# Four chained cross-attention layers: sums by products with ones in odd grouped steps alone, and ScalarE's copy of a grouped half ahead of the last masked exponentials

## The chip, the core and the metric

The kernel runs on one core of a Trainium2 chip. The core has a matrix engine (TensorE, PE in the profile, with its weight loads shown as PEld), a vector engine (VectorE, DVE), an activation engine (ScalarE, ACT), a general engine (GpSimd, POOL) and a queue that issues transfers (SyncE, SP). Each engine works through its own instructions in the order in which they stand, and waits for others by semaphores. Matrix products land in PSUM, eight banks of 128 x 512 fp32, from where ScalarE or VectorE takes them to SBUF. The metric is the device time of one launch in microseconds, the median of the timed runs.

## The reference

A state x (4 batches of 512 positions, 256 channels) goes through four cross-attention layers over one context per batch (1024 positions, 512 channels). Layers 0, 2 and 3 are alike: 16 heads of 64, a bias on the columns of a few tokens that comes from two masks over the 512 positions, softmax, product with the values, output projection, bias and residual.

```python
q = hidden_states @ Wq; k = encoder_hidden_states @ Wk; v = encoder_hidden_states @ Wv
logits = einsum('bhqd,bhkd->bhqk', q, k) * scale + col_bias
probs = softmax(logits, axis=-1)
out = einsum('bhqk,bhkd->bhqd', probs, v) @ Wo + bo + residual
```

Layer 1 normalises x by its root mean square and has 16 heads of 16 with 4 shared key and value heads, without masks. All is computed in fp32.

## The kernel before

**Units and steps.** The work is cut into units: the units of layers 0, 2 and 3 ("masked" units), eight to a layer and batch, two heads each; and the units of layer 1 ("grouped" units), also eight to a batch. The main loop (L1227) runs over steps. A step takes one masked unit `g`, and in four stretches of eight steps, one for each batch, a grouped unit `lam` beside it. In the step in which `lam` is attended, the logits of the next grouped unit, `coming`, are made. A grouped unit has a half `h`: units 0, 2, 4, 6 (`h == 0`) stand in what are called even steps here, units 1, 3, 5, 7 in odd steps. `tabled[0]` is true in a step that has both `lam` and `coming`, so for units 0 to 6 of each batch: 28 steps of the 32.

**Tiles.** The logits of a unit are eight blocks of 128 x 1024 (context positions by two heads of 512 queries). All the rest goes over these: copy to SBUF, maximum, subtraction, exponential in place, products with the values.

**A step in the order of the code.**
- POOL subtracts the maximum from the blocks of `lam` (L952).
- TensorE makes the scores of `g` (`scores`, L849), ScalarE copies each block to SBUF (L859), VectorE takes maxima (L906 and the small operations to L946).
- TensorE attends the masked unit of the step before, `g1` (`attend`, L882).
- Then a list `fill` of matrix work is run: output projections (L1086), queries (L746), keys of the next masked units (L540) in odd steps or values (L588) in even steps. Beside it, ScalarE and VectorE get their work from a list `events`: each entry has a time in microseconds of estimated matrix work, and `pass_events(us)` issues what lies before it. For `g` these are eight subtractions (L954) at 0.7 + 1.2 t and eight exponentials (L960) at 3.3 + 1.22 t, with a running sum on POOL behind each exponential (L999). After each piece of matrix work that leaves a result to be copied, the loop calls `pass_events(now)` and then issues the copy (L1443 to L1447).
- Where the estimates in `fill` pass 9.5, `attend_grouped` (L1392) is put in: the attention of `lam` (L882, tiles of 32 columns). It returns `keep_even` (L887), so the loop first issues the exponentials that are due and then ScalarE's copy of one half of the result into `o` (L892). VectorE's addition of the other half, `keep_odd` (L896), is put on the list `late`; in odd steps `turn_grouped` (L1001 to L1015) too.
- The logits of `coming` follow in four pairs of blocks (`logits_pair`, L822), with a piece of `fill` between two pairs. Each pair takes two places of two banks; `Place` (L109) picks among banks 0 to 3 in these steps, so a pair uses the banks of the pair before. ScalarE copies both blocks (L828), VectorE takes their maxima (L906). Before the first pair, `behind_exponentials` (L1299) issues all remaining events and then what is on `late`.

**The sums of the softmax.** For `g1` the running sum of its exponentials is added over 128 partitions. There are two ways. `sums_beside` (L1050) does it with two matrix products with ones (L1054), put in `fill` in front of `attend_grouped`; VectorE then turns one row over, takes the reciprocal and turns it back (L785 to L787). `reciprocal_sums` (L1024) does it on VectorE alone: a reduction over the running sum (L906, on the tile `st`), seven small operations (L1031 to L1036), the reciprocal (L1040) and one turn (L1042). Both end in `scale_out` (L1068), and both are on `late`. `by_ones` (L1320) picks the first way; before the change it holds in all 28 steps.

## Time and profile before

| | us |
|---|---|
| timed runs | 3494.37, 3494.56, 3499.84; median 3494.56 |
| profiled execution | 3500.28 |
| its span, first to last instruction | 3498.5 |
| TensorE busy | 3447.4 |
| VectorE busy | 2964.0 |
| POOL busy | 2491.6 |
| ScalarE busy | 2336.4 |
| granted TensorE clock, mean | 0.996 |

A row of the costliest groups or of a timeline gives line, engine, operation, tiles, shapes and count. In the timelines here the columns are: start in us from the span's start, length in us, engine, line, operation, result and source, count of instructions merged into the row, and in brackets the idle time before it and what ended it. A list of waits has: who waited, for whom, the total in us, how often, and the longest. An fp32 matrix product shows as two instructions. Matrix products are pipelined, so the length of a row of them reaches a little into the next one; differences of starts are what the engine needed.

### The profile page before, as it was taken

Reading aid. Unit: us, or ns where it says so; the run is one execution under the profiler, and the core shown is the slowest. Engines: PE = TensorE matmul, PEld = TensorE weight load, DVE = VectorE, ACT = ScalarE, POOL = GpSimd, SP = SyncE. Lnnn points to the kernel's source line nnn. Section 1 sums busy time; section 2 is a strip of 40 time slices with the busy share of each in tenths; the row PEclk is TensorE's granted clock in tenths of the full one; section 3 lists DMA queues with packets and bytes.
Section 4 is the critical chain, followed back from the end, with each engine's and each line's share of the span. In section 5 each row is a group of like instructions: output and inputs, shape, how many; then the busy total and the mean of one; then the engine's idle time right before and its main releaser. Section 6 shows DMA issues by size and latency. Waiting matters only on the chain.

```text
span 3498.5 us, 42340 instructions
## 1 busy us (share of the span) xinstructions
PE 3447.4 (99%) x15374; PEld 1673.5 (48%) x15374; DVE 2964.0 (85%) x3898; ACT 2336.4 (67%) x2701; POOL 2491.6 (71%) x1241
## 2 busy tenths in 40 slices
PE   8999999999999999999999999999999999999998
PEld 4454444444444454444545455454544445454553
DVE  7778788887888878898888888888788888889887
ACT  4565577775777757776666666666577766666664
POOL 3665577884888848887777768777488877769774
PEclk9999999999999999999999999999999999999999
DMA  3223211002100120001001011011101101011010
GB/s 104 64 73 107 63 32 50 26 23 74 43 28 28 37 82 29 26 29 44 28 28 52 25 34 52 28 52 43 48 29 50 35 20 52 28 39 59 31 32 7
DMA packets 146198, 151.69 MB, mean 43 GB/s; under 512 B 23608, under 2 KB 123448, under 8 KB 145476
## 3 DMA queue, kind: packets, MB, share of 16 engines
q1 hardware_dynamic: 142894, 140.05, 12.7%
q0 software_dynamic: 2560, 8.39, 0.8%
q8 instruction: 122, 2.00, 0.2%
q14 instruction: 88, 0.72, 0.1%
q10 hardware_dynamic: 534, 0.52, 0.0%
HBM read 132.15 MB, written 15.73 MB: 42 GB/s over the span
## 4 chain that ended last, share of the span: by engine, by line
PE 88%; DVE 8%; ACT 2%; POOL 1%; issue 1%; DMA 0%; DVEq 0%; ACTq 0%; POOLq 0%
PE ps L882 19%; PE ps L849 17%; PE ps L643 13%; PE ps L588 11%; PE ps L540 10%; PE ps L746 5%; PE ps L822 4%; PE ps L1086 4%; DVE tops L906 2%; DVE st L954 2%; DVE ps L866 1%; POOL st L952 1%; ACT st L828 1%; PE ps L723 1%; PE ps L1054 1%
## 5 line engine op out<-in xcount | busy, mean ns | idle before, releaser
L999 POOL TENSOR_TENSOR st<-st 128x1024 f32<-128x1024 f32 x668 | 1581.7, 2368 | 682.3 <-ACT st L960 637.4
L960 ACT ACTIVATE st<-st 128x1024 f32<-128x1024 f32 x1024 | 1040.1, 1057 | 330.7 <-DVE st L954 188.4
L954 DVE TENSOR_TENSOR st<-st,ps 128x1024 f32<-128x1024 f32 x768 | 883.2, 1214 | 3.3
L952 POOL TENSOR_TENSOR st<-st 128x1024 f32<-128x1024 f32 x256 | 598.1, 2381 | 281.9 <-DVE st L946 281.9
L882 PE MATMUL ps<-st,v 128*64 128x512 f32 (+1 forms) x4064 | 791.3, 597 | 4.7 <-ACT kt L545 4.7
L866 DVE TENSOR_TENSOR ps<-ps,st 128x1024 f32<-128x1024 f32 x476 | 586.7, 1233 | 246.3 <-ACT st L859 202.9
L859 ACT COPY st<-ps 128x1024 f32<-128x1024 f32 x768 | 714.6, 1050 | 67.4 <-PE ps L855 51.3
L849 PE MATMUL ps<-qt,kt 64*128 64x512 f32 x3072 | 710.6, 600 | 10.5 <-DVE every L933 8.3
L906 DVE TRANSPOSE_TENSOR_REDUCE tops<-st 128x32 f32<-128x1024 f32 x448 | 517.7, 1211 | 55.8 <-ACT st L828 55.3
L882 PEld LDWEIGHTS ps<-st,v 128*64 128x64 f32 (+1 forms) x4064 | 240.1, 130 | 541.1 <-issue 456.1
L849 PEld LDWEIGHTS ps<-qt,kt 64*128 64x128 f32 x3072 | 285.0, 186 | 377.0 <-ACT st L859 153.9
L540 PE MATMUL ps<-ctx,wk 128*128 128x512 f32 x896 | 414.4, 610 | 2.2 <-ACT ctx L420 2.2
L588 PE MATMUL ps<-wv,ctx 128*128 128x256 f32 x1792 | 405.9, 382 | 0.0
L588 PEld LDWEIGHTS ps<-wv,ctx 128*128 128x128 f32 x1792 | 336.2, 190 | 96.7 <-issue 48.0
L828 ACT COPY st<-ps 128x1024 f32<-128x1024 f32 x256 | 247.2, 1017 | 108.0 <-PE ps L822 107.7
L540 PEld LDWEIGHTS ps<-ctx,wk 128*128 128x128 f32 x896 | 168.4, 193 | 236.8 <-issue 220.3
L643 PE MATMUL ps<-st 128*128 128x128 f32 (+1 forms) x1200 | 228.9, 339 | 5.2 <-ACT ps L666 5.2
L658 ACT COPY st<-ps 128x512 f32<-128x512 f32 x40 | 23.4, 586 | 301.6 <-PE ps L643 301.6
L643 PEld LDWEIGHTS ps<-st 128*128 128x128 f32 x1200 | 158.8, 192 | 73.4 <-issue 66.2
L746 PE MATMUL ps<-x,wq 128*128 128x512 f32 x384 | 186.6, 609 | 1.1 <-ACT x L383 1.1
L822 PE MATMUL ps<-qt,kt 32*128 32x512 f32 x1024 | 170.1, 640 | 8.7 <-ACT st L828 8.3
L1086 PE MATMUL ps<-ot,wo 128*128 128x512 f32 x384 | 175.8, 600 | 0.7 <-DVE ot L1068 0.7
(184 smaller groups left out, 2694.8 us busy)
## 6 DMA issues: line engine op xcount, KB each, us to landing
ctx<-kept SPq DMA_DIRECT2D x24, 1024.0 KB, 8.1
wk<-in_L_xattn_Wk_dram SPq DMA_DIRECT2D x47, 512.0 KB, 3.5
wv<-in_L_xattn_Wv_dram SPq DMA_DIRECT2D x47, 512.0 KB, 3.4
wq<-in_L_xattn_Wq_dram SPq DMA_DIRECT2D x96, 128.0 KB, 3.5
wo<-in_L_xattn_Wo_dram SPq DMA_DIRECT2D x96, 128.0 KB, 3.5
st<-kept SPq DMA_DIRECT2D x4, 2048.0 KB
qt<-q SPq DMA_DIRECT2D x64, 128.0 KB, 3.5
kept<-st SPq DMA_DIRECT2D x12, 512.0 KB, 3.2
```

The lines of the kernel that those rows point to most:

```text
L540: nc.tensor.matmul(m, lhsT=g.w["k"][:, k, :], rhs=ctx_half[g.b, n][:, k, :], start=(k == 0), stop=(k == KT - 1),)
L588: nc.tensor.matmul(m[:, half * 2 * P : (half + 1) * 2 * P], lhsT=ctx_half[g.b, t // 4][:, k, t % 4 * P : (t % 4 + 1) * P], rhs=g.w["v2"][: ...
L643: nc.tensor.matmul(m if is_keys else m[:, q], lhsT=right[:, k, :] if is_keys else left_[:, k, q], rhs=left_[:, k, :] if is_keys else right ...
L849: nc.tensor.matmul(m[:, j * S : (j + 1) * S], lhsT=g.kt[g.rows[j], keys], rhs=g.qt[g.rows[j], :], start=True, stop=t > 0,)
L859: nc.scalar.copy(g.st[t], m)
L866: nc.vector.tensor_tensor(top, top, g.st[t], ALU.max)
L882: nc.tensor.matmul(g.po[at, :], lhsT=g.v[:, t, rows], rhs=g.st[t][:, j * S : (j + 1) * S], start=(t == first), stop=(t == last),)
L906: nc.vector.tensor_reduce(out_, of.rearrange("p (b x) -> p b x", x=32), AX.X, op, apply_transpose=True)
L952: nc.gpsimd.tensor_tensor(g.st[t], g.st[t], g.mb, ALU.subtract)
L954: nc.vector.tensor_tensor(g.st[t], g.st[t], g.mb, ALU.subtract)
L960: nc.scalar.activation(st, st, AF.Exp)
L999: nc.gpsimd.tensor_tensor(g.acc, g.st[0] if t == 1 else g.acc, g.st[t], ALU.add)
```

## The change

Two edits in the main loop. The products with ones are used only where the grouped unit that is attended has `h == 1`; in the even steps of the 28 the sums of `g1` go by `normalise` (`reciprocal_sums` and `scale_out`). And `attend_grouped` no longer returns `keep_even` for the loop to issue behind the events that are due; it issues events up to 8.6 itself (subtractions to block 6, exponentials to block 4) and then the copy at once. The exponentials of blocks 5 to 7 that have not been issued by then follow the copy.

```diff
-        by_ones = tabled[0]
+        by_ones = tabled[0] and lam.h == 1
...
                 late.append(lambda: keep_odd(lam))
                 if lam.h == 1:
                     late.append(lambda: turn_grouped(lam))
-                return lambda: keep_even(lam)
+                pass_events(8.6)
+                keep_even(lam)
```

In the instruction order of the two programs this is: TensorE has 16 pairs of products with ones less and is otherwise unchanged; VectorE has ten instructions in place of three at 16 places; ScalarE's copy L892 stands in front of three exponentials (L960) that it followed before, in all 32 steps but seven, where it is one (unit 4 of each batch) or two; POOL's and SP's order is the same.

## The prediction

> **What bounds the kernel now.** I read the page first: busy shares, then the chain that ended last.

> ```profile
> PE 3447.4 (99%) x15374; PEld 1673.5 (48%) x15374; DVE 2964.0 (85%) x3898; ACT 2336.4 (67%) x2701; POOL 2491.6 (71%) x1241
> ...
> PE 88%; DVE 8%; ACT 2%; POOL 1%; issue 1%; DMA 0%; DVEq 0%; ACTq 0%; POOLq 0%
> ```

> TensorE idles 51 of 3498.5 us and carries 88% of the chain, so work taken from it should count, unless something makes it wait. Next, the waits, for who stands between the engines around the grouped unit:

> ```profile
> DVE o L896 <- ACT o L892: 48.5, 28, 2.7
> ...
> PEld ps L822 <- ACT st L828: 47.6, 62, 2.3
> ```

> VectorE waits 48.5 us for the half copy (L892) that the change moves forward. TensorE in its turn waits for the pair copies (L828), which stand behind L892 on ScalarE. So the timelines of an even step (unit 2 of batch 0), TensorE then ScalarE then VectorE:

> ```profile
> 559.65 1.08 PE L1054 MATMUL ps<-st,ones 128*64 128x512 f32 x4
> 560.66 3.64 PE L882 MATMUL ps<-st,v 128*32 128x512 f32 x32
> 564.23 1.14 PE L822 MATMUL ps<-qt,kt 32*128 32x512 f32 x8
> 565.30 1.99 PE L588 MATMUL ps<-wv,ctx 128*128 128x256 f32 x8
> 567.23 1.34 PE L822 MATMUL ps<-qt,kt 32*128 32x512 f32 x8
> 568.50 1.99 PE L588 MATMUL ps<-wv,ctx 128*128 128x256 f32 x8
> ```
> ```profile
> 560.14 2.96 ACT L960 ACTIVATE st<-st 128x1024 f32<-128x1024 f32 x3
> 564.37 0.58 ACT L892 COPY o<-ps 64x512 f32<-64x512 f32 x1 [1.27 <-PE ps L882]
> 565.46 1.93 ACT L828 COPY st<-ps 128x1024 f32<-128x1024 f32 x2 [0.51 <-PE ps L822]
> ```
> ```profile
> 560.78 0.72 DVE L785 STREAM_TRANSPOSE ot<-ps 128x512 f32<-128x512 f32 x1 [1.88 <-PE ps L1054]
> ...
> 564.98 0.69 DVE L896 TENSOR_TENSOR o<-o,ps 64x512 f32<-64x512 f32 x1 [1.72 <-ACT o L892]
> ```

> See three things. ScalarE does its three exponentials while TensorE still runs the grouped attention, and only then waits for it. VectorE is idle 1.88 + 1.72 us. And the second pair (567.23) has to wait for the first pair's copies, since both use banks 0 to 3: TensorE goes on at 568.50, which is 3.04 us after the first copy's start. The odd step (unit 3) has the same constant, with an open wait:

> ```profile
> 604.36 1.46 PE L822 MATMUL ps<-qt,kt 32*128 32x512 f32 x8
> ...
> 609.17 2.04 PE L822 MATMUL ps<-qt,kt 32*128 32x512 f32 x8 [1.43 <-ACT st L828]
> 611.14 3.64 PE L540 MATMUL ps<-ctx,wk 128*128 128x512 f32 x4
> ```
> ```profile
> 604.52 2.95 ACT L960 ACTIVATE st<-st 128x1024 f32<-128x1024 f32 x3
> 607.50 0.58 ACT L892 COPY o<-ps 64x512 f32<-64x512 f32 x1
> 608.10 1.93 ACT L828 COPY st<-ps 128x1024 f32<-128x1024 f32 x2
> ```

> Here 611.14 - 608.10 = 3.04 again. So the moment the first pair copy starts sets TensorE.

> **The change part by part.**

> *Sums in the 16 even steps, TensorE.* One pair of products with ones goes: 560.66 - 559.65 = 1.01 us, and TensorE runs without a gap from there to 607. By itself: 16 x 1.01 = 16.2 us less.

> [...] I go by the gapless rows.

> *Sums, VectorE.* Three instructions (0.72 + 0.25 + 0.71, with gaps 1.79) become ten, ahead of the same L1068. The row of unit 7, which has them already, runs from 778.83 (L906) to 782.56 (L1068): 3.73. Extra 1.94 us, 31.0 in all. In the even step it no longer waits for the products: its last subtraction ends at 558.9, so sums, scaling and all end near 563.4 to 564.7 (the bank for the reduction is the one ScalarE empties until 560.24). Then it needs the half copy, then the pair copies; both come later, so the cover is the 3.6 us of idle above. If that cover were gone, 1.94 a step. I take 0. It can't go below nothing either: what ends earlier on VectorE here only waits longer for the half copy at L896.

> *Half copy ahead of the exponentials.* The copy needs the end of the grouped attention; what is now queued behind that wait is three exponentials (one in the four units 4, two in two odd steps and one unit 7, by the instruction order of the two programs), and behind them the pair copies that TensorE needs. Even step, unit 2: TensorE ends the attention at 564.23 - 1.01 = 563.22; the copy starts 0.14 later (564.37 - 564.23); 0.60 to the next instruction (607.50 to 608.10); three exponentials 2.98 (604.52 to 607.50); the first pair copy starts at 566.94, not 565.46. Plus 3.04: TensorE goes on at 569.98, not 568.50, so it is **1.48 us later**, though 1.01 of work has gone. Nothing gives that back: the later pairs follow at the same distance, and the next step's VectorE and POOL work starts from the last pair. Worth it per kind:
> - units 0, 2, 6, twelve steps: eleven x 1.48 = 16.3; unit 0 of batch 1, where the first copy was at 908.06 and the attention's end at 906.56, comes to 909.27: 1.2.
> - unit 4, four steps: two of the exponentials already stand ahead, one (1.04) comes behind: attention's end 652.03 - 1.01 + 0.14 + 0.60 + 1.04 = 652.80 against 653.26: -0.46, -1.8 in all.
> - unit 5, four steps: nothing was taken from TensorE; attention's end 693.79 + 0.14 + 0.60 + 2.98 = 697.51 against 695.89: 1.62 each, 6.5.
> - units 1 and 3, eight steps: in six the attention ends when ScalarE arrives (604.36 + 0.14 = 604.50 against 604.52), so copy and exponentials only trade places: 0. In unit 1 of batch 1 and unit 3 of batch 3 TensorE came late to the attention, waiting for a key copy (L545): 950.96 + 0.14 + 0.60 + 2.0 = 953.70 against 952.19, 1.5; 2688.16 + 2.74 = 2690.90 against 2689.44, 1.5.
> - unit 7, four steps: no pair follows; the key copies come up to 1.7 later (784.97 for 783.27), but TensorE's next product rows stand unbroken from 781.25 with other banks free: 0, at most 1.7.

> What VectorE wins: its add (L896) and in odd steps the four grouped operations run up to 1.7 us sooner. That is worth nothing if it next waits for a pair copy, and it does (idle before L906 in all: 55.3 us, for L828). POOL's running sums come to the late exponentials 0.5 us after they are ready (three of 2.43 us from 558.19 put block 5's add at 565.5, its exponential ends at 565.0); were they late, nobody reads them before the next step. DMA: no issue moves or is added; SP's and POOL's queues keep their order.

> *Sum.* 16.3 + 1.2 - 1.8 + 6.5 + 1.5 + 1.5 = +25.2 us, the 16.2 already inside (the forward copy alone would be 41.4). The profiled execution took 3500.28 us, so its like would take 3525.5; it stands 5.7 above the median of the timed runs, 3494.56, and I add the difference to the median: **3519.8 us**.

> Unknown, with both ends: how long after TensorE's end the copy starts when ScalarE is already waiting, 0.14 in the row that waited 1.27; a floor is the block that the copy reads last, one of eight earlier (3.57 / 8 = 0.45): 22 steps x 0.45 = 10 less. I take 0.14, the same wait. And the six ties: from 0 to 0.6 each if TensorE slips by a copy's length, 3.6 more. I take 0, as both sides of the tie start from the same pair.

> **The rivals.**
> *Faster, the wait is hidden.* Place: the second pair. If TensorE could issue it before the copies, the 16.2 would stay whole: 3478.4. The point that decides: the first copy must start by 565.46 to break even, which leaves 565.46 - 563.96 = 1.50 for exponentials behind the half copy: one gains, two lose. For it: TensorE idles for L828 seldom today. Against: 3.04 in both steps shown, with and without an idle gap.
> *Faster, VectorE sets the odd steps.* The chain runs on VectorE from 575.7 to 606.4. If it did so after, too, twelve odd steps x 1.71 and 16.2 make 36.7: 3457.8. Against: the chain goes on over ScalarE's exponential, L892 and L828, whose sum in front of 608.10 stays the same.
> *About the same.* The late pair is made up in ScalarE's pauses (1.27 and 0.54 us between the later pairs) before the next step. Then the even steps cost nothing and save nothing, unit 5 likewise: within 7 us of 3494.6. Against: TensorE, not ScalarE, would have to catch up, and it has no pause.
> *Slower still.* VectorE's cover fails in the twelve steps, 23.3 more: 3543.

> **How the numbers follow.** My sum 0.77; slower still 0.09; about the same 0.06; hidden 0.05; VectorE 0.03. The sum's own range is 3510 (0.45 earlier) to 3530 (ties 3.6, units 7 up to 6.8). Wider by 5 for the spread of the runs (3494.37 to 3499.84), which also reaches a little into the slower case, it holds 8 in 10: 3504 to 3535. A measurement of this kernel tells about 0.2%, 7 us. Slower 0.86, same 0.06, faster 0.08.

> **What will show it.** L1054 x48 instead of x112; L785 gone from the even steps, L1031 to L1042 there. ScalarE's wait at L892 for L882, 8.6 us in all today, grows to some 45 us: 2.4 in twelve even steps, 1.6 in the units 5, the rest in the units 7 and the two late odd steps. TensorE is idle about 1.8 us before the second pair in twelve even steps (arrival 566.22, start some 1.07 after the first copy). VectorE's wait at L896 gone from most steps, and moved to L906. I am wrong if in unit 2 the first pair copy starts before the last exponential, or TensorE goes on less than 6 us after the attention's end.

## The result and the profile after

The changed kernel takes 3534.41 us (median of 4 runs, 3530.31 to 3537.66), the kernel before 3497.2 beside it: a ratio of 1.0105, 95% interval 1.0093 to 1.0117. The profiled execution takes 3535.15 us, its span is 3533.4, against 3500.28 and 3498.5 before: +34.9, where the sum of the prediction was +25.2. The mean granted clock (the share of full speed that the profile shows as granted to TensorE) fell from 0.996 to 0.990. The kernel is slower by about 1%, clear of the noise.

The page of the changed kernel, busy shares and the chain that ended last:

```profile
PE 3458.9 (98%) x15310; PEld 1678.5 (48%) x15310; DVE 2992.8 (85%) x4010; ACT 2332.4 (66%) x2701; POOL 2490.0 (70%) x1241
...
PE 89%; DVE 4%; ACT 4%; POOL 1%; issue 1%; DMA 0%; DVEq 0%; ACTq 0%; POOLq 0%
```

TensorE has 64 instructions less and is busy 11.5 us longer. That is the first thing to explain: waits lengthen its idle time (74.5 us now, 51.1 before), but less work should not lengthen its busy time.

The waits of the kernel before, then of the changed kernel (who, for whom, total us, times, longest):

```profile
ACT o L892 <- PE ps L882: 8.6, 16, 1.3
...
PE ps L822 <- ACT st L828: 8.3, 6, 1.4
```
```profile
DVE tops L906 <- ACT st L828: 96.6, 77, 4.4
...
PEld ps L822 <- ACT st L828: 80.8, 77, 2.4
...
ACT o L892 <- PE ps L882: 46.7, 26, 3.1
...
PE ps L822 <- ACT st L828: 33.2, 24, 1.6
```

ScalarE now waits 46.7 us at the half copy, 8.6 before. TensorE waits 33.2 for pair copies, 8.3 before, and 24 times, six before. Its weight loads wait for them 80.8, 47.6 before; that wait lies inside the second pair, between its two blocks, and counts as busy in a merged row (2.04 for 1.34 us), which is part of the longer busy time.

The step that the prediction worked through, unit 2 of batch 0, TensorE, then ScalarE, then VectorE:

```profile
565.72 1.14 PE L822 MATMUL ps<-qt,kt 32*128 32x512 f32 x8
566.79 1.99 PE L588 MATMUL ps<-wv,ctx 128*128 128x256 f32 x8
570.24 2.04 PE L822 MATMUL ps<-qt,kt 32*128 32x512 f32 x8 [1.45 <-ACT st L828]
572.20 1.99 PE L588 MATMUL ps<-wv,ctx 128*128 128x256 f32 x8
```
```profile
565.86 0.58 ACT L892 COPY o<-ps 64x512 f32<-64x512 f32 x1 [3.11 <-PE ps L882]
566.34 2.95 ACT L960 ACTIVATE st<-st 128x1024 f32<-128x1024 f32 x3
569.19 1.90 ACT L828 COPY st<-ps 128x1024 f32<-128x1024 f32 x2
```
```profile
562.85 1.26 DVE L906 TRANSPOSE_TENSOR_REDUCE ps<-st 128x32 f32<-128x1024 f32 x1 [1.45 <-ACT v L595]
...
566.58 0.69 DVE L1068 TENSOR_TENSOR ot<-ps,ot 128x512 f32<-128x512 f32 x1
567.30 0.69 DVE L896 TENSOR_TENSOR o<-o,ps 64x512 f32<-64x512 f32 x1
570.22 4.67 DVE L906 TRANSPOSE_TENSOR_REDUCE tops<-st 128x32 f32<-128x1024 f32 x4 [2.23 <-ACT st L828]
```

ScalarE stands 3.11 us at L892 until the attention ends (565.72), copies, does the three exponentials, and only then takes the first pair. TensorE goes on at 572.20, 6.48 us after the attention's end; before it was 4.27. The sums on VectorE wait 1.45 us at their own start, are done before the pair copy comes, and VectorE waits 2.23 us more for that copy.

**Step by step.** For each of the 32 grouped steps I took how much later the next step's scores (L849) start than in the kernel before, less the same for the step before it. Some single steps are off by about 1.70 us or twice that, either way; apart from that, each kind of step gives one number to 0.1 us: units 0, 2 and 6 +1.1 to +1.21 (unit 0 of batch 1 +0.93), unit 4 -0.69, unit 5 +1.42 to +1.49, units 1, 3 and 7 nothing within 0.1, but +1.5 and +1.3 in the two late odd ones. Together +19.8. The steps of 1.70 add up to the rest, some 15.

**Where the 1.70 comes from.** A gap is a stretch in which TensorE runs nothing. The windows of the changed kernel around two of them (stretch, length, busy time and instructions of PE, PEld, DVE, ACT, POOL, then granted clock, DMA share, GB/s), and TensorE's rows in the second:

```profile
478.00:486.00 8.00, 7.32 (x27) 4.05 (x28) 4.67 (x4) 4.35 (x6) 6.57 (x3) 0.79 0.00 0
522.00:530.00 8.00, 7.05 (x21) 2.27 (x22) 5.95 (x6) 4.37 (x7) 7.76 (x4) 0.79 0.09 33
```
```profile
519.58 1.98 PE L540 MATMUL ps<-ctx,wk 128*128 128x512 f32 x4
522.95 2.04 PE L822 MATMUL ps<-qt,kt 32*128 32x512 f32 x8 [1.39 <-ACT st L828]
524.92 3.68 PE L540 MATMUL ps<-ctx,wk 128*128 128x512 f32 x4
```

The kernel before has the same pattern at the same place:

```profile
520.50 2.10 PE L822 MATMUL ps<-qt,kt 32*128 32x512 f32 x8 [1.41 <-ACT st L828]
522.53 3.58 PE L540 MATMUL ps<-ctx,wk 128*128 128x512 f32 x4
```

In the changed kernel the same four instructions of L540 take 1.98 us ahead of the gap and 3.68 behind it. The clock is at one half for 3.41 us (0.79 over 8 us is 1 - 0.5 x 3.41 / 8; the window 525.06:528.47 shows 0.50), which costs 1.70 us of TensorE's work. In the record of the granted clock between 400 and 2950 us, where the grouped steps lie, the kernel before has 7 such stretches (23.9 us), the changed one 14 (54.6 us, two of them doubled). Half of the difference, (54.6 - 23.9) / 2 = 15.3 us, is lost. So the steps and the clock make 19.8 + 15.3 = 35.1 us, against 34.9 measured.

### The profile page after: what moved, and what is told of

It is laid out like the page before. It is cut to its first block, busy times and chain, and to the rows that moved or that the text cites. A ratio compares the mean times of both kernels' runs of the same rounds, so it can differ in the third digit from the quotient of the medians.

```text
span 3533.4 us, 42334 instructions
## 1 busy us (share of the span) xinstructions
PE 3458.9 (98%) x15310; PEld 1678.5 (48%) x15310; DVE 2992.8 (85%) x4010; ACT 2332.4 (66%) x2701; POOL 2490.0 (70%) x1241
## 3 DMA queue, kind: packets, MB, share of 16 engines
q8 instruction: 121, 1.98, 0.2%
## 4 chain that ended last, share of the span: by engine, by line
PE 89%; DVE 4%; ACT 4%; POOL 1%; issue 1%; DMA 0%; DVEq 0%; ACTq 0%; POOLq 0%
PE ps L882 20%; PE ps L849 18%; PE ps L643 13%; PE ps L540 11%; PE ps L588 10%; PE ps L822 5%; PE ps L746 5%; PE ps L1086 4%; ACT st L960 2%; POOL st L952 1%; DVE ps L866 1%; ACT st L828 1%; DVE st L954 1%; PE ps L855 1%; PE ps L723 1%
## 5 line engine op out<-in xcount | busy, mean ns | idle before, releaser
L960 ACT ACTIVATE st<-st 128x1024 f32<-128x1024 f32 x1024 | 1040.7, 1057 | 332.0 <-DVE st L954 187.9
L882 PE MATMUL ps<-st,v 128*64 128x512 f32 (+1 forms) x4064 | 793.2, 599 | 4.7 <-ACT kt L545 4.7
L849 PE MATMUL ps<-qt,kt 64*128 64x512 f32 x3072 | 710.6, 599 | 8.8 <-DVE every L933 6.5
L906 DVE TRANSPOSE_TENSOR_REDUCE tops<-st 128x32 f32<-128x1024 f32 x448 | 518.1, 1212 | 97.3 <-ACT st L828 96.6
L882 PEld LDWEIGHTS ps<-st,v 128*64 128x64 f32 (+1 forms) x4064 | 240.6, 130 | 536.4 <-issue 464.5
L849 PEld LDWEIGHTS ps<-qt,kt 64*128 64x128 f32 x3072 | 285.5, 186 | 374.8 <-ACT st L859 153.1
L540 PE MATMUL ps<-ctx,wk 128*128 128x512 f32 x896 | 417.2, 613 | 2.2 <-ACT ctx L420 1.1
L588 PE MATMUL ps<-wv,ctx 128*128 128x256 f32 x1792 | 413.7, 387 | 0.0
L588 PEld LDWEIGHTS ps<-wv,ctx 128*128 128x128 f32 x1792 | 340.9, 193 | 99.8 <-issue 43.1
L828 ACT COPY st<-ps 128x1024 f32<-128x1024 f32 x256 | 246.5, 1013 | 113.3 <-PE ps L822 113.2
L540 PEld LDWEIGHTS ps<-ctx,wk 128*128 128x128 f32 x896 | 168.9, 194 | 239.3 <-issue 223.4
L643 PE MATMUL ps<-st 128*128 128x128 f32 (+1 forms) x1200 | 228.9, 339 | 5.1 <-ACT ps L666 5.1
L822 PE MATMUL ps<-qt,kt 32*128 32x512 f32 x1024 | 184.8, 653 | 33.2 <-ACT st L828 33.2
L643 PEld LDWEIGHTS ps<-st 128*128 128x128 f32 x1200 | 158.8, 192 | 73.4 <-issue 64.0
```

The source lines that it names most:

```text
L540: nc.tensor.matmul(m, lhsT=g.w["k"][:, k, :], rhs=ctx_half[g.b, n][:, k, :], start=(k == 0), stop=(k == KT - 1),)
L588: nc.tensor.matmul(m[:, half * 2 * P : (half + 1) * 2 * P], lhsT=ctx_half[g.b, t // 4][:, k, t % 4 * P : (t % 4 + 1) * P], rhs=g.w["v2"][: ...
L643: nc.tensor.matmul(m if is_keys else m[:, q], lhsT=right[:, k, :] if is_keys else left_[:, k, q], rhs=left_[:, k, :] if is_keys else right ...
L849: nc.tensor.matmul(m[:, j * S : (j + 1) * S], lhsT=g.kt[g.rows[j], keys], rhs=g.qt[g.rows[j], :], start=True, stop=t > 0,)
L882: nc.tensor.matmul(g.po[at, :], lhsT=g.v[:, t, rows], rhs=g.st[t][:, j * S : (j + 1) * S], start=(t == first), stop=(t == last),)
L906: nc.vector.tensor_reduce(out_, of.rearrange("p (b x) -> p b x", x=32), AX.X, op, apply_transpose=True)
```

## Experiments

The medians of the kernel before lay between 3497.1 and 3498.4 us beside the experiments. "Half clock" is the time at half clock between 400 and 2950 us in the profiled execution.

| run | median us | ratio to before, 95% | half clock, us |
|---|---|---|---|
| sums alone | 3476.45 | 0.9932, 0.9916 to 0.9949 | 10.2 |
| copy alone | 3557.76 | 1.0155, 1.0133 to 1.0177 | 68.3 |
| one exponential behind | 3483.87 | 0.9957, 0.994 to 0.9973 | 6.8 |
| two behind | 3500.82 | 1.0013, 1.0003 to 1.0022 | 13.7 |
| no products at all | 3489.34 | 0.9977, 0.9967 to 0.9987 | 44.4 |
| gap filled, first try | 3556.06 | 1.017, 1.0151 to 1.0188 | 51.2 |
| gap filled, second try | 3562.97 | 1.0197, 1.0181 to 1.0212 | 47.8 |
| longer piece in the gap | 3513.22 | 1.0043, 1.0029 to 1.0057 | 6.8 |
| longer piece elsewhere | 3571.18 | 1.021, 1.0192 to 1.0228 | 54.6 |
| copy behind the pair | 3478.48 | 0.9945, 0.9927 to 0.9963 | 6.8 |
| the same, odd steps alone | 3473.34 | 0.9938, 0.9925 to 0.9952 | 0 |
| and one exponential later | 3468.49 | 0.9919, 0.9906 to 0.9933 | 6.8 |

### The two edits apart

The sums alone (against the kernel before):

```diff
-        by_ones = tabled[0]
+        by_ones = tabled[0] and lam.h == 1
```

> Only the first edit: in even steps the sums go by VectorE, the half copy stands where it stood. Theory (TensorE is bound by when the first pair copy starts; the forward copy alone made the loss): the attention of the grouped unit ends 1.01 us sooner in 16 even steps, and the pair copies follow, except where ScalarE's exponentials then end later than the attention (idle before the half copy was 0.43 or 0.25 us, so 0.8 to 0.93 is left): about 14 us less, 3483 of a median of 3497. Rival (VectorE's extra 1.94 us a step is on the path): 0 to 31 us more, 3497 to 3528.

The copy alone (against the changed kernel):

```diff
-        by_ones = tabled[0] and lam.h == 1
+        by_ones = tabled[0]
```

> Only the second edit: products with ones in all 28 steps, the half copy ahead of the exponentials. Theory: even steps of units 0, 2 and 6 lose 0.14 + 0.48 + 2.85 + 3.01 - 4.27 = 2.2 us each (26 us), units 4 lose 0.3, units 5 1.5, two late odd steps 1.4 each: 36 us. Theory of the clock: every idle of TensorE of over 1.2 us can be followed by 3.4 us at half clock, 1.7 us lost; as many as in the changed kernel (15 against 7 in the stretch) add 14 us: 3547 in all. Rival (the two edits are bad only together): near 3497.

Sums alone: apart from the clock's 1.70, the even steps are 1.00 to 1.04 us shorter, but for unit 0 of batch 1 (0.54) and the first, which holds all that differs ahead of it (1.57); the expectation had 0.8 to 0.93 for some of them. The odd ones stay. TensorE in unit 2, with no gap between the first and the second pair:

```profile
559.98 1.14 PE L822 MATMUL ps<-qt,kt 32*128 32x512 f32 x8
561.05 1.99 PE L588 MATMUL ps<-wv,ctx 128*128 128x256 f32 x8
562.97 1.34 PE L822 MATMUL ps<-qt,kt 32*128 32x512 f32 x8
```

Copy alone: units 0, 2 and 6 come 2.21 later, unit 4 0.32, unit 5 1.47: the changed kernel's 1.21 and -0.69 with the 1.01 put back, and unit 5 as it was. ScalarE stands 4.12 us at the copy:

```profile
567.93 0.58 ACT L892 COPY o<-ps 64x512 f32<-64x512 f32 x1 [4.12 <-PE ps L882]
```

So the first edit gains and the second loses more. Both runs go further than the waits: half clock falls to 10.2 us in the one and rises to 68.3 in the other.

### How many exponentials may stand behind the copy

Against the changed kernel, one and two in place of three:

```diff
-                pass_events(8.6)
+                pass_events(10.7)      # one behind;  9.5 for two
```

> Both edits, but only the exponential of block 7 stands behind the half copy. Theory: in all 16 even steps the first pair copy starts at 0.14 + 0.48 + 0.95 = 1.57 us after the attention's end, which came 1.01 sooner: 0.7 us less a step, 11 us less; odd steps unchanged: 3486. Rival (any copy ahead of exponentials makes ScalarE lose its wait of 2 to 3 us): slower than 3497.

> Both edits, with the exponentials of blocks 6 and 7 behind the half copy. Theory: 0.14 + 0.48 + 1.9 + 3.01 - 1.01 = 4.52 against 4.27: 0.25 us more in twelve even steps, 0.7 less in the four units 4 (one behind there), 0.4 more in units 5, 1.4 in two late odd steps: 5 us more, 3502, and up to 7 us from half clocks. So the sign turns between one and two exponentials. Rival (the loss is the same wherever the copy stands ahead): near 3534.

ScalarE in unit 2 with one behind, then with two:

```profile
562.22 0.58 ACT L892 COPY o<-ps 64x512 f32<-64x512 f32 x1 [1.20 <-PE ps L882]
562.70 1.05 ACT L960 ACTIVATE st<-st 128x1024 f32<-128x1024 f32 x1
563.66 1.90 ACT L828 COPY st<-ps 128x1024 f32<-128x1024 f32 x2
```
```profile
560.73 0.58 ACT L892 COPY o<-ps 64x512 f32<-64x512 f32 x1 [2.15 <-PE ps L882]
561.21 2.00 ACT L960 ACTIVATE st<-st 128x1024 f32<-128x1024 f32 x2
563.12 1.90 ACT L828 COPY st<-ps 128x1024 f32<-128x1024 f32 x2
```

From copy to pair copy it is 1.44 and 2.39 us, and 3.33 in the changed kernel (565.86 to 569.19): 0.95 for each exponential. The steps of units 0, 2 and 6 follow: -0.69, +0.26, +1.21 against the kernel before; with none behind, the run above, -1.01. The sign turns between one and two.

### Is it the gap that halves the clock?

Two tries put 1.01 us of unused products into the gap before the second pair in the even steps of the changed kernel (this adds work that the result does not use), the first in a bank that `Place` gave, the second in one picked by hand:

```diff
+            if i == 1 and lam and lam.h == 0:
+                w = Place(1)          # second try: a bank above 3, taken past Place
+                for j in range(2):
+                    nc.tensor.matmul(w.ap[coming.rows[j], :], lhsT=ones[:, 0:64], rhs=coming.qt, start=True, stop=True)
+                w.back()
```

> The changed kernel with an unused pair of products with ones (1.01 us, nothing reads them) in each even step in the idle time ahead of the second pair of logits, so that TensorE idles 0.44 instead of 1.45 us there. Theory of the clock (idle of over 1.2 us brings half clocks): the waits stay as they are, since the second pair waits for the copies anyway, but the half clocks that come in even steps go, some 5 to 8 of 1.7 us: 8 to 13 us less than the changed kernel, 3521 to 3526, though it does more work. Rival (the half clocks have nothing to do with the idle time): 3534 again.

> The changed kernel, with a pair of products of ones and queries (1.01 us, read by nobody) ahead of the second pair of logits in the even steps, written to a bank above 3 that was given back last; the choice of banks for all other work is untouched. It adds work that the result does not use. Theory (the idle gap before the second pair brings the stretches at half clock): the second pair starts when it did, the gap falls from about 1.45 to 0.45 us, no new wait appears in the steps, and the half clock stretches that begin in even steps go; 5 to 8 of them at 1.7 us each, so 3520 to 3526. Rival (the clock falls for another reason, for instance by time or by load): gap smaller, as many half clock stretches as in the changed kernel (14, of which two double), about 3534.

Both missed. TensorE of the first try, then of the second, around unit 2:

```profile
573.50 2.03 PE L822 MATMUL ps<-qt,kt 32*128 32x512 f32 x8 [0.44 <-ACT st L828]
...
587.00 5.40 PE L849 MATMUL ps<-qt,kt 64*128 64x512 f32 x16 [2.11 <-DVE every L933]
```
```profile
573.18 1.31 PE L1311 MATMUL ps<-qt,ones 128*64 128x512 f32 x4 [2.84 <-ACT v L595]
```

In the first the gap did fall to 0.44, but `Place` gives the bank that came back longest ago, so the extra request changed the banks of all that followed, and a wait of 2.11 us arose in the next scores. In the second the bank was still being copied by ScalarE (L595), so the gap grew to 2.84. Neither tests the gap.

What does: the piece of values or keys between the first and the second pair gets two of its products twice, in its own bank and ahead of the right ones (work that the result does not use; no other instruction is added and no bank changes). A control does the same with the piece between the third and the fourth pair, where TensorE has no gap.

```diff
+        for k in range(2 if twice[0] else 0):       # v_pair; likewise in k_part
+            nc.tensor.matmul(..., start=True, stop=True)
...
             logits_pair(coming, i)
+            twice[0] = bool(lam and i == 0)          # i == 2 in the control
```

> The changed kernel, with two of the products of the piece of keys or values between the first and the second pair of logits done twice (1.0 us, in the bank that the piece owns, the first result overwritten) in all 28 steps that have pairs. It adds work and changes no other instruction. Theory (the idle gaps before the second pair bring the half clock): the second pair starts when it did, the gaps of 1.4 to 1.6 us become 0.4 to 0.6, and the 11 half clock stretches that begin behind such gaps go, three behind other waits stay: 54.6 us at half clock become some 10 to 17, so 19 to 22 us less; against it 3 us where the gap was smaller (unit 4, and two units 2 and 4): 3515 to 3519 in spite of 56 products more. Rival (the clock falls by itself, or by the load): half clock stretches as before, 3534 to 3540.

> The same 56 products, in the piece between the third and the fourth pair, where TensorE has no gap. Theory: each costs what it takes, 28 x 0.8 to 1.0 us on top of the changed kernel, with its gaps and its half clock stretches (12 to 16) kept: 3555 to 3563. If it came out near the run before it, the place of the products, and so the gap, would not be what matters.

With 56 products more, the first takes 3513.22 us, 21.2 less than the changed kernel; the second, with the same 56, takes 3571.18. The first, TensorE in unit 2 and the window over the step where the changed kernel stood at 0.79 (its lines from 588 on are numbered up to 16 higher: L604 is L588, L838 is L822, L844 is L828, L598 the products done twice):

```profile
563.12 1.13 PE L598 MATMUL ps<-wv,ctx 128*128 128x256 f32 x4
564.09 1.89 PE L604 MATMUL ps<-wv,ctx 128*128 128x256 f32 x8
566.56 2.03 PE L838 MATMUL ps<-qt,kt 32*128 32x512 f32 x8 [0.59 <-ACT st L844]
568.53 1.99 PE L604 MATMUL ps<-wv,ctx 128*128 128x256 f32 x8
```
```profile
475.00:483.00 8.00, 7.41 (x39) 4.49 (x36) 6.70 (x7) 6.55 (x8) 7.77 (x4) 1.00 0.00 1
```

TensorE goes on 6.48 us after the attention's end (568.53 - 562.05), just as in the changed kernel, so the wait is the same; the gap is 0.59 for 1.45, and the clock stays at 1.00. Half clock falls from 54.6 us to 6.8; the two stretches left stand behind other waits, in a unit 7 and a late odd step. (54.6 - 6.8) / 2 = 23.9 us, less 0.34 in each unit 4, is the 21.9 by which the profiled spans differ, but for 0.6. The control keeps the gap of 1.45 us and the half clock (3.78 us for the 1.99 of the same piece):

```profile
477.93 2.63 PE L838 MATMUL ps<-qt,kt 32*128 32x512 f32 x8 [1.45 <-ACT st L844]
480.49 3.78 PE L604 MATMUL ps<-wv,ctx 128*128 128x256 f32 x8
```

It came out above its expectation. Apart from the clock's 1.70, its steps are about 0.66 us longer than in the changed kernel where the piece is one of values (16 steps), and, where it is one of keys, 1.7 in units 1 and 3 and 1.5 in unit 5, not 0.8 to 1.0. That makes 30 us, as in the profiled spans (30.1; both have 54.6 us at half clock), and its median lies 6 above its profiled execution. That short gaps bring the half clock, and that this cost the change some 15 us, is shown by this pair of runs.

### Should the odd steps lose their products too?

```diff
-        by_ones = tabled[0]
+        by_ones = False
```

> Sums by VectorE in all 28 steps, the half copy as before the change. Theory (in odd steps ScalarE's exponentials set the first pair copy, so that TensorE's 1.01 us less only turns into idle time): the same as sums in the even steps alone, 3476, plus up to 10 us for half clocks, as the idle time ahead of the second pair in odd steps grows from 1.4 to 2.4 us. Rival (TensorE's work counts in all steps): 12 us less, 3464. Rival (VectorE is what ends the odd steps): 1.94 x 12 = 23 us more, 3499.

It is 13 us slower than the sums alone (3489.34 for 3476.45; its profiled execution, at 3494.56, is among the slowest of its ten), although TensorE has twelve pairs of products less. TensorE in unit 3 and the window over unit 1:

```profile
602.28 1.98 PE L540 MATMUL ps<-ctx,wk 128*128 128x512 f32 x4
606.29 2.04 PE L822 MATMUL ps<-qt,kt 32*128 32x512 f32 x8 [2.03 <-ACT st L828]
```
```profile
520.00:530.00 10.00, 10.00 (x30) 3.56 (x29) 9.25 (x10) 5.86 (x7) 6.22 (x3) 0.83 0.07 26
```

In the odd steps the pair copy is set by ScalarE, as the prediction read it, so the work taken from TensorE only became gap (2.03 for 1.39), and the half clock rose from 10.2 to 44.4 us, which is 17 of the difference in the profiled spans (17.1).

### The half copy the other way, behind the pair copies

If ScalarE's queue ahead of L828 sets the step, the half copy itself can leave it. First in all steps, on top of the sums alone (in unit 7, which has no pair, behind all remaining events); then in units 1, 3 and 5 only; then there with the last block's exponential behind the second pair's copies as well. The edit of the second and third run:

```diff
-        by_ones = tabled[0]
+        by_ones = tabled[0] and lam.h == 1
...
             logits_pair(coming, i)
+            for each in behind.pop(i, ()):
+                each()
...
+                if lam.h == 1 and coming:
+                    behind[0] += [lambda: keep_even(lam), lambda: keep_odd(lam), lambda: turn_grouped(lam)]
+                    pass_events(10.7)                          # third run only
+                    behind[1] += [each[2] for each in events]  # third run only
+                    events.clear()                             # third run only
+                    return
```

> Sums by VectorE in even steps, and the half copy moved the other way: behind the first pair's two copies, VectorE's additions of the grouped unit behind the pair's maxima. Theory (the start of the first pair copy sets TensorE): in odd steps it comes 0.6 us sooner, 12 x 0.6 = 7 us less than with the sums alone, 3469, and some half clocks less; in even steps nothing more than 0.2 each. Rival (the half copy holds up something else, VectorE's grouped maxima in their turn): no better than 3476, or worse.

> The kernel before with the sums by ones in odd steps alone, and in units 1, 3 and 5 the half copy, VectorE's addition and the four grouped operations behind the first pair's copies; even steps and units 7 as in the kernel before but for the sums. Theory (in odd steps ScalarE alone sets the first pair's copy, and the half copy is 0.74 us of it, as the run with the copy behind the pair showed): 12 odd steps 0.74 earlier, even steps as with the sums alone: 3476.5 - 8.9 = about 3468. Rival (the moved addition delays VectorE's maxima and gives it back in the next step): 3474 to 3478.

> As the run before it, and in the same units the exponential of the last block (1.0 us) behind the second pair's copies. Theory (ScalarE's queue ahead of the first pair's copy sets the odd steps, until the end of the grouped attention does): another 0.9 to 1.0 us in units 1 and 3 and little in unit 5, where the attention ends later: some 8 us, about 3460, and fewer gaps before the second pair, so fewer half clock stretches. Rival (the exponential delays the later copies, or the running sum of the masked unit comes late for the attention in the next step): no better than the run before it.

In all steps it gains nothing (3478.48): the odd steps are 0.74 shorter (0.6 was expected), but most even ones 0.23 longer, and in unit 7, where the copy went behind the key copies, VectorE waits for it:

```profile
DVE o L896 <- ACT o L892: 26.8, 4, 8.3
```

In odd steps alone (0.9938) it can't be told from the sums alone (0.9932). The odd steps win 0.71 to 0.76 each and most units 2, 4 and 6 behind them give 0.70 back: VectorE now has the addition and the four grouped operations between the pair's maxima and is the late one.

```profile
690.02 0.69 DVE L896 TENSOR_TENSOR o<-o,ps 64x512 f32<-64x512 f32 x1
...
693.17 6.87 DVE L906 TRANSPOSE_TENSOR_REDUCE tops<-st 128x32 f32<-128x1024 f32 x6
```

These six maxima run without a pause, so the next step's first maximum comes 3.10 us earlier than with the sums alone (703.23 for 706.33), where TensorE's scores come 3.99 earlier (699.42 for 703.41). The third run is the fastest of all, 3468.49, 0.9919 of the kernel before. Units 1 and 3 are mostly 1.65 to 1.70 shorter than with the sums alone; TensorE and ScalarE in unit 3:

```profile
597.55 1.75 PE L822 MATMUL ps<-qt,kt 32*128 32x512 f32 x8
599.23 1.98 PE L540 MATMUL ps<-ctx,wk 128*128 128x512 f32 x4
601.15 1.46 PE L822 MATMUL ps<-qt,kt 32*128 32x512 f32 x8
```
```profile
597.61 2.01 ACT L960 ACTIVATE st<-st 128x1024 f32<-128x1024 f32 x2
599.52 1.91 ACT L828 COPY st<-ps 128x1024 f32<-128x1024 f32 x2
...
604.35 1.08 ACT L960 ACTIVATE st<-st 128x1024 f32<-128x1024 f32 x1
```

The pair copy comes while TensorE still works at L540, and there is no gap. About half of what the odd steps win is still returned in units 2, 4 and 6, 0.7 each, as in the run before it.

## Why the prediction was right, and where it was not

- **What sets the step** (the first pair copy's start, TensorE going on 3.04 us behind it): right. It is 3.01 in the changed kernel with a gap in front, and the order L892, three exponentials, L828 came as written.
- **Sums, 16 x 1.01 on TensorE**: right, to 0.03 in 14 of the 16 steps of the run with the sums alone. That run is 22.8 us shorter in its profiled span, 16 of it from the steps and 6.8 from less half clock, so the gapless rows that the prediction went by held in this kernel.
- **Sums on VectorE at nothing**: right. With the sums alone the even steps lose none of their 1.01, and in the changed kernel VectorE still waits 2.23 us for the pair copy behind them.
- **Half copy, units 0, 2, 6: 1.48 each**: right in mechanism, too large by 0.27. The hand-over from the copy to an exponential took 0.48 for the 0.60 read from copy to copy, three exponentials to the pair copy 2.85 for 2.98, and the rest 3.01 for 3.04. A duration read ahead of one kind of successor was used for another. The same shows, with 0.15 to 0.23, in unit 4 (-0.69 for -0.46) and unit 5 (1.47 for 1.62). All twelve, four and four steps and the two late odd ones: 19.8 us for 25.2.
- **Ties in units 1 and 3, unit 7 at nothing**: right, within 0.1 but for the clock's steps.
- **The unknown start of the copy** (0.14, or up to 0.45 earlier): 0.14 it was, 565.86 against 565.72.
- **The missing term**: the prediction listed the idle gap before the second pair (about 1.8 us; 1.45 it became) as a sign, and priced it at its own length alone. "Nothing gives that back" was true, but a gap of this length was also followed by half clock in a good third of the cases (53 of 148 gaps of 1.3 to 1.8 us, the table at the end). The trace of before had it in full view: the 3.58 us of L540 at 522.53 behind the gap of 1.41, and the rows that the prediction itself quotes, 609.17 with 1.43 idle and 611.14 with 3.64 us for four instructions that take 1.98 elsewhere. That row was used for its start and not read for its length. Worth 15.3 us.
- **Luck in the number**: the time, 3534.41, lay 0.6 below the upper end of the range, 3535. The upper part of the range had been meant for ties, for unit 7 and for the spread of the runs; ties and unit 7 came to nothing. The forecast of 3519.8 was 14.6 short: 15.3 from the half clock, less 5.4 from the hand-overs, and the other 5 because the profiled execution of before stood 5.7 above its median and that of the changed kernel only 0.7. Had the hand-overs been sized right, forecast and range would have stood 5.4 lower and ended near 3529.6, and the time would have lain outside. The waits were understood; that the number held was luck.
- **Rivals**: "Hidden" needs the exponentials behind the half copy to take no more than 1.50 us; one takes 0.95 and gains, two take 1.9 and lose, as the prediction said. "VectorE sets the odd steps" (3457.8) is out, since odd steps with a tie did not move, and "about the same" is out, since units 0, 2 and 6 lost 1.1 to 1.21 each and made none of it up. "Slower still" had a time near the measured one for a wrong reason: the cover did not fail.

## What to carry to other kernels

Moving a short copy forward on an in-order queue moves its wait in front of all that stands behind it (ScalarE's 3.11 us at L892 in unit 2 here); count what may stand between the wait's end and the next thing the bounding engine needs (here one exponential, not two). Work taken from an engine only counts where no other queue sets its next start (1.00 to 1.04 us a step in most even steps here); where one does, the work was filling a gap (2.03 for 1.39 us in unit 3 without any products with ones), and a gap on TensorE may cost more than itself (1.70 us of clock behind one of 1.39 in the changed kernel). In the trace of before, look for the same merged row with two lengths. The longer one held either a wait (2.04 for 1.34 us at L822) or a lowered clock (3.68 for 1.98 at L540) here; the granted clock of a short window tells which (0.50 in 525.06:528.47), and what stands ahead of the second kind shows what brings it on.

## What the hardware showed that was not expected

| gap, us | gaps | followed by half clock |
|---|---|---|
| 0.3 to 1.0 | 98 | 0 |
| 1.0 to 1.3 | 53 | 2 |
| 1.3 to 1.8 | 148 | 53 |
| over 1.8 | 71 | 44 |

These 99 are all the stretches between 400 and 2950 us. Each is 3.41 or 6.83 us long (the kernel before has seven of 3.41, the changed one twelve of 3.41 and two of 6.83), and within each of the 13 executions that have any, their starts lie on a grid of 3.4133 us to a hundredth: in the kernel before from 522.36 to 2604.49, 610 x 3.4133, and in the changed one from 480.69 to 2856.36, 696 x 3.4133. Whether a gap of 1.4 us was followed by the 1.7 us lost went with how it fell on that grid and with what stood behind it. Of 104 gaps of 1.38 to 1.59 us ahead of the second pair in these 13, 53 were followed by half clock: all 52 that began from 0.57 us before to 0.96 us after a point of the grid, one of the two at 1.04, and none of the 50 that began 1.05 to 2.8 us after one. In the changed kernel it was 11 of 21, in the kernel before 4 of 5. The 40 other gaps of 1.3 to 1.8 us, ahead of scores or the products of L643, were never followed, wherever they fell. The idle time in the 3.41 us ahead of a point of the grid alone does not separate the cases (0.9 to 2.8 us where the clock fell, up to 2.0 where it did not). What sets the grid is not shown. Why the pair makes a difference stays open; its products read 32 partitions (32x512 in its rows), the products of other rows 64 or 128, and no run varies that.
